# Layer 0, first convolution: two classes of row pairs interleaved in each frame, written in adjacent elements and read every second one

## The chip, the cores and the metric

The kernel runs as one program on one core of a Trainium2 chip. Its time is what the device takes for one execution, in microseconds (us). Five engines matter here: TensorE (PE in the profile; PEld is its weight load), VectorE (DVE), ScalarE (ACT), GpSimd (POOL) and SyncE (SP), which issues most DMA transfers. A difference of 0.2% of the time, about 10 us, can be told from no change.

## What is computed

A stack of four residual layers on `x`, shape (4, 16, 512, 512), float32. The change lies in layer 0, so only that layer is given in full:

```python
def _denoise_block(x, w1, b1, w2, b2, w3, b3, a, b, c):
    trip = _triplets(x)                      # frames t-1, t, t+1 (mirrored at the ends)
    B, T, C, H, W = trip.shape
    xf = trip.reshape(B * T, C, H, W)
    o = a * _conv_reflect(xf, w1, b1, 1, 2) + b * _conv_reflect(xf, w2, b2, 2, 4) \
      + c * _conv_reflect(xf, w3, b3, 4, 8)  # three 5x5 convolutions, dilation 1, 2, 4
    return jnp.tanh(o).reshape(B, T, H, W)
...
x = x + denoise_block_2(denoise_block_1(_gn(x)))   # layer 0
x = x + conv3x3(quantized(_gn(x)))                 # layer 1
x = x + box17x17(_gn(x))                           # layer 2
x = x + irfft2(complex_conv3x3(rfft2(_gn(x))))     # layer 3
```

`_gn` normalises groups of two of the sixteen frames (channels) over the whole image.

## The kernel before

Layer 0 is class `Layer0`. Its two convolutions (`conv` 0 and 1, blocks 1 and 2 of the reference) are worked as 32 groups: conv 0 for the four batches, four output frames at a time, then conv 1 in the same way. A group takes six slots, one for each of the six products over time: six combinations `v[q]` of the input frames are formed on VectorE (`early`, `late`; lines 487 to 551), each is convolved in space on TensorE (`products`, line 579), and the six results are combined into four output frames (`gather`, lines 626 to 647). The 96 slots of conv 0 come first, the 96 of conv 1 after them. `slot` writes the order by hand: TensorE's products of a slot, then on the other engines the results of the slot before, and the frames and combinations that the next group needs. Every engine works its list in that order.

**A frame** is a tile of 128 partitions by 2376 elements (line 87, ten of them, taken from a list of free ones). A patch of 2 rows by 16 columns stands in 32 partitions; the image's four quarters (128 rows each) stand in the four groups of 32 partitions. Along the free axis of a conv 0 frame there are 33 column blocks `k` of 72 elements. The 64 row pairs of a quarter are sorted by their number modulo 4 into four classes of 16, and each class has one more element at either end, the rim, which holds the row pair of the neighbouring quarter: 4 x 18 = 72.

**Making a conv 0 frame** is `x_frame`. For each half `h` of the frame's rows, ScalarE normalises the raw rows into `xp` (line 399) and mirrors 8 columns at each side (lines 400, 401); VectorE transposes blocks of 32 x 32 from `xp` into the frame (line 432, 1056 elements in each partition). In such a block a partition's number in its quarter is `2m + u`, with `m` from 0 to 15 and `u` 0 or 1, so one transpose delivers two classes, `u` = 0 and 1, of the half `h`. ScalarE then copies the rims from the transposed tile `ek`, 132 elements for each side (line 436). A group of conv 0 makes four frames, the first of a batch five: 64 frames in all, 128 transposes.

**The products** read the frames. One product takes a pair of displacements `d`, `d + 1` (in row pairs); for each column block its moving operand is two runs of 16 elements, one of the class that `d` leads to and one of the class of `d + 1`, for 16 column blocks: 16 x 2 x 16 = 512 columns. `source` gives the address. `PAIRS` lists five `d` whose two weight blocks lie side by side, so that one product fills 64 output columns (32*64 in the profile, "wide" below); `ALONE` lists the displacements that are worked 32 columns at a time (32*32, "narrow"), two of them beside each other. The four groups of partitions (`i`) and two halves of the columns (`j`) run as separate tiles of the array at once: eight wide instructions or sixteen narrow ones fill it. Each float32 product is two instructions in the profile. A slot thus has 160 wide and 128 narrow instructions, wide first in even slots and narrow first in odd ones, so that two slots together have 40 rounds of eight wide ones in a row.

Conv 1 has frames of another layout, loaded by DMA (`y_frame`); there the runs are 32 elements long.

Of the kernel before, what the change touches and what calls it, by code (L numbers as in the profile page):

```python
# [122 lines left out]
class Layer0:  # L123
# [299 lines left out]
    def x_frame(self, b, t, raws, ek, f):  # L423

        nc = self.nc
        fr = self.free.pop(0)
        v = fr.rearrange("p (k u c m) -> p k u c m", u=2, c=2, m=18)
        scale, bias, _ = self.gn[b]
        for h in range(2):
            raw = raws[h].rearrange("p (s w) -> p s w", s=2)  # L430
            xp = self.normalised(raw, scale[:, t : t + 1], bias[:, t : t + 1], f"{b}_{t}_{h}")
            nc.vector.transpose(v[:, :, :, h, 1:17].rearrange("p k u m -> p k m u"), xp)  # L432
        rim = ek.rearrange("p k (e f m) -> p k e f m", e=2, f=4)
        v = fr.rearrange("p (k q m) -> p k q m", q=4, m=18)
        for side in range(2):
            nc.scalar.copy(v[:, :, :, 17 * side], rim[:, :, side, f, :])
        return fr

    def y_frame(self, gr, i, t):
# [119 lines left out]
    def products(self, gr, p):  # L559
        nc, conv, q = self.nc, gr["conv"], ORDER[p]  # L560
        ps = self.psum.tile([P, 4, 512], F32, name=f"m{self.now}", tag="m")
        v = gr["v"][q]
        w = self.w[q]
        runs = [(e, pair) for e in range(2) for pair in PAIRS], [(e, two) for e in range(2) for two in ALONE]
        order = [(wide, *what) for wide in ((1, 0) if p % 2 == 0 else (0, 1)) for what in runs[1 - wide]]

        def source(i, d, k, j):
            if conv:
                a = [1188 * (c % 4 // 2) + 66 * (c % 2) + 1 + c // 4 for c in (d, d + 1)]
                first, step, nk, nm = 132 * k + 32 * j, 132, 8, 32  # L570
            else:
                a = [18 * (c % 4) + 1 + c // 4 for c in (d, d + 1)]
                first, step, nk, nm = 72 * (k + 16 * j), 72, 16, 16
            o = v[PX * i : PX * i + PX]
            return bass.AP(o.tensor, o.offset + first + a[0], [o.ap[0], [step, nk], [a[1] - a[0], 2], [1, nm]])

        def product(at, i, weights, d, e, j, n):
            nc_ = 8 if conv else 16
            return nc.tensor.matmul(  # L579
                ps[at, i, :].rearrange("p (k c m) -> p k c m", k=nc_, c=2),  # L580
                w[PX * i : PX * i + PX, weights],
                source(i, d, e, j),
                start=(n == 0),
                stop=(n == len(order) - 1),
                skip_group_check=True,
            )

        for n, (wide, e, what) in enumerate(order):
            base = len(DELTA) * PX * e
            for i in range(4):  # L590
                for j in range(2):
                    if wide:
                        d, o = what
                        at = base + PX * o
                        ins = product(slice(64 * j, 64 * j + 64), i, slice(at, at + 64), d, e, j, n)
                        continue
                    for u, (d, o) in enumerate(what):
                        at = base + PX * o
                        out = slice(64 * j + PX * u, 64 * j + PX * u + PX)
                        ins = product(out, i, slice(at, at + PX), d, e, j, n)  # L600
            self.marks.append(ins.ins)
        gr["m"][q] = ps
# [1187 lines left out]
```

## Time and profile before

| What | Value |
|---|---|
| time, median of 3 runs | 5083.87 us (5082.6 to 5091.45) |
| time of the profiled execution | 5071.62 us |
| its span on the core | 5069.8 us |
| ACT busy | 2564.1 us (51%) |
| products of layer 0 (L579), PE busy | 2610.4 us in 55296 instructions |
| combining frames (L487, 128x2376), DVE busy | 607.9 us in 232 instructions |
| transposes into the frames (L432), DVE busy | 261.6 us in 128 instructions |
| rim copies (L436), ACT busy | 43.5 us in 128 instructions |
| DMA: read, written | 497.51 MB, 340.03 MB |

The span covers the profiled execution from its first to its last instruction; the 1.8 us that the execution takes beyond it lie around the program. The profiled execution was 12.3 us faster than the median of the runs. Busy times of an engine are sums over the whole span; conv 0 of layer 0 takes roughly the first 28% of it, conv 1 the next 27%. In a line of instruction groups the shape is partitions x elements, `x128` the number of instructions, then the sum of their busy time in us, the mean of one in ns, and the idle time before them with what ended it.

### The profile page before, as it was taken

The page shows a single profiled execution, that of the slowest core. Times are in us where ns is not written, and L with a number is a line of the kernel's source. Part 1 is how long each engine was busy: PE and PEld are TensorE (multiplying, and loading weights), DVE is VectorE, ACT ScalarE, POOL GpSimd, SP SyncE. Part 2 cuts the span into 40 slices and gives each one's busy share as a digit, 9 for nine tenths or more (in the row PEclk, how much of TensorE's full clock was granted, in tenths as well). Part 3 has the DMA queues.
Part 4 walks back from the last instruction along what each step waited for, and adds up shares of the span by engine and source line. Part 5 has one row for each costly group of instructions (what it writes and reads, how often), then busy time and mean ns, then how long its engine had stood idle before and what let it go on. Part 6 is the DMA issues. An engine that isn't in the chain of part 4 may idle for free.

```text
span 5069.8 us, 209515 instructions
## 1 busy us (share of the span) xinstructions
PE 4765.5 (94%) x94320; PEld 2775.5 (55%) x94320; DVE 4070.7 (80%) x4639; ACT 2564.1 (51%) x4220; POOL 21.4 (0%) x90
## 2 busy tenths in 40 slices
PE   4899999999999989999999699989999989999999
PEld 1344444444554434444444456558888857777776
DVE  8988888979689999999998565555555588888887
ACT  3455656563224443534443555445444456666665
POOL 0000000000000000000000000000000000000000
PEclk9999999999999999999999899999999989999999
DMA  5655655564567776877774777776666655555553
GB/s 173 164 163 160 178 162 162 150 167 103 124 144 162 148 153 153 169 153 149 167 155 116 218 232 240 228 232 216 214 215 211 200 136 150 142 148 148 143 151 114
DMA packets 393857, 851.22 MB, mean 168 GB/s; under 512 B 70912, under 2 KB 86400, under 8 KB 384512
## 3 DMA queue, kind: packets, MB, share of 16 engines
q1 hardware_dynamic: 385456, 827.22, 61.0%
q8 instruction: 739, 12.11, 1.1%
q10 hardware_dynamic: 7504, 10.60, 0.8%
q14 instruction: 158, 1.29, 0.1%
HBM read 497.51 MB, written 340.03 MB: 165 GB/s over the span
## 4 chain that ended last, share of the span: by engine, by line
PE 78%; DVE 14%; issue 3%; DMA 2%; ACT 2%; SPq 1%; ACTq 0%; POOL 0%; DVEq 0%
PE m L579 39%; PE l1p L1044 11%; PE l2p L1151 8%; PE u L1619 5%; PE s L1560 5%; PE u L1560 4%; DVE frame L487 4%; PE u L1582 2%; PE pt L1594 2%; DVE frame L432 2%; DVE l2o L1191 2%; PE l2p L1202 1%; DVE st L1192 1%; DVE B L630 1%; DVE A L631 1%
## 5 line engine op out<-in xcount | busy, mean ns | idle before, releaser
L579 PE MATMUL m<-frame,l0w 32*64 32x512 f32 (+1 forms) x55296 | 2610.4, 610 | 174.8 <-DVE frame L527 63.4
L579 PEld LDWEIGHTS m<-frame,l0w 32*64 32x64 f32 (+1 forms) x55296 | 1193.9, 119 | 1590.4 <-issue 1361.8
L487 DVE SCALAR_TENSOR_TENSOR frame<-frame,frame 128x2376 f32<-128x2376 f32 x232 | 607.9, 2628 | 8.6
L1044 PE MATMUL l1p<-l1q,l_wt 32*32 32x512 f32 x12288 | 481.3, 601 | 64.6 <-DVE l1q L1034 40.4
L1044 PEld LDWEIGHTS l1p<-l1q,l_wt 32*32 32x32 f32 x12288 | 263.0, 103 | 229.2 <-issue 151.1
L1191 DVE TENSOR_TENSOR l2o<-l2x,l2p 128x512 f32<-128x512 f32 x256 | 172.7, 675 | 267.0 <-PE l2p L1151 267.0
L712 ACT ACTIVATE junk<-xb,neg 128x1024 f32<-128x1024 f32 x256 | 293.6, 1147 | 82.8 <-DVE top L691 36.5
L1151 PEld LDWEIGHTS l2p<-k_c_band,l2y 128*128 128x128 f32 x2048 | 256.8, 190 | 76.0 <-issue 55.2
L1180 ACT COPY l2y<-l2p 128x512 f32<-128x512 f32 x256 | 149.9, 586 | 284.2 <-PE l2p L1151 284.2
L1151 PE MATMUL l2p<-k_c_band,l2y 128*128 128x144 f32 (+1 forms) x2048 | 284.3, 292 | 6.1
L432 DVE STREAM_TRANSPOSE frame<-xp 128x1056 f32<-128x1056 f32 x128 | 261.6, 2128 | 31.1 <-ACT xp L401 31.1
L1151 PE MATMUL l2p<-k_c_band,l2n 128*128 128x144 f32 (+1 forms) x2048 | 269.7, 292 | 13.7 <-ACT l2n L1169 10.4
L1151 PEld LDWEIGHTS l2p<-k_c_band,l2n 128*128 128x128 f32 x2048 | 263.0, 197 | 14.7 <-ACT l2n L1169 10.9
L1061 DVE BATCH_NORM_STATS2 l1st<-l1o 128x6 f32<-128x512 f32 x256 | 158.2, 681 | 135.0 <-ACT l1o L1059 134.9
L1059 ACT ACTIVATE l1o<-l1p,k_l_bias,l_osc 128x1024 f32<-128x1024 f32 x128 | 147.2, 1200 | 233.6 <-PE l1p L1044 227.8
L1619 PE MATMUL u<-k_c_hil,zt 128*128 128x128 f32 x2048 | 255.9, 278 | 0.0
L1619 PEld LDWEIGHTS u<-k_c_hil,zt 128*128 128x128 f32 x2048 | 238.4, 192 | 2.1 <-issue 0.8
L1595 ACT COPY zt<-pt 128x512 f32<-128x512 f32 x256 | 131.4, 599 | 209.5 <-PE pt L1594 209.5
L1525 DVE TENSOR_TENSOR xc<-l3n,k_c_tab 128x2048 f32<-128x2048 f32 x64 | 146.7, 2293 | 106.6 <-ACT l3n L1509 106.6
L1638 DVE SCALAR_TENSOR_TENSOR l3o<-u,l3t 128x256 f32<-128x256 f32 x512 | 192.2, 426 | 22.2 <-ACT l3t L1630 19.5
L1044 PE MATMUL l1p<-l1x,l_wt 32*32 32x512 f32 x4088 | 194.6, 597 | 0.0
L1630 ACT ACTIVATE l3t<-u,rr 128x128 f32<-128x128 f32 x512 | 152.3, 362 | 70.3 <-DVE rr L1613 53.5
(314 smaller groups left out, 6351.3 us busy)
## 6 DMA issues: line engine op xcount, KB each, us to landing
y<-y SPq DMA_DIRECT2D x256, 264.0 KB
xb<-in_x SPq DMA_DIRECT2D x512, 128.0 KB
x<-l1o SPq DMA_DIRECT2D x256, 256.0 KB
l2x<-x SPq DMA_DIRECT2D x64, 1024.0 KB
x<-l2o SPq DMA_DIRECT2D x64, 1024.0 KB
l3x<-x SPq DMA_DIRECT2D x256, 256.0 KB
out<-l3o SPq DMA_DIRECT2D x256, 256.0 KB
l1x<-x SPq DMA_DIRECT2D x252, 256.0 KB
```

The costliest lines, as they stand in the source:

```text
L432: nc.vector.transpose(v[:, :, :, h, 1:17].rearrange("p k u m -> p k m u"), xp)
L487: self.nc.vector.scalar_tensor_tensor(o, x, f, y, ALU.mult, ALU.add)
L579: return nc.tensor.matmul(ps[at, i, :].rearrange("p (k c m) -> p k c m", k=nc_, c=2), w[PX * i : PX * i + PX, weights], source(i, d, e, j) ...
L712: nc.scalar.activation(junk, xs[h], f, bias=neg, accum_out=self.out_sums[b][n][:, 2 * t + h : 2 * t + h + 1])
L1044: ins = nc.tensor.matmul(ps[32 * j : 32 * j + 32, b, :], wt[rows, a, d], qs[v % 3][rows, k, d : d + W] if d < 3 else raws[v][rows, k], sta ...
L1061: nc.vector.bn_stats(st[b][:, u, :], o[:, b, :])
L1151: nc.tensor.matmul(ps[:, lo:hi], lhs[:, k, at : at + P], band[:, j : j + hi - lo], start=(k == 0), stop=(k == 3), skip_group_check=True,)
L1191: nc.vector.tensor_add(o[:, hb, :], xt[:, hb, :], ps)
L1560: nc.tensor.matmul(ps[b][32 * j : 32 * j + 32], f[rows, n, j, :], x[rows, j, :], start=(i == 0), stop=(i == 2 and tag == "s"), skip_group_ ...
L1619: nc.tensor.matmul(po[:, bass.ts(k, P)], zt[:, b, k ^ 1, :], hil[:, k, :], start=False, stop=(k == 3), skip_group_check=True,)
L1630: nc.scalar.activation(t[:, cols], po[:, cols], AF.Identity, bias=rr[:, b, odd : odd + 1], scale=0.5)
L1638: nc.vector.scalar_tensor_tensor(o[:, v].rearrange("p k u -> p u k"), po[:, HW:W].rearrange("p (u k) -> p u k", u=2), s, t.rearrange("p (u ...
```

## The change

Two classes that differ in `u` now alternate element by element: a column block of 72 elements is 2 (`c`, the half `h`) x 18 (`m`) x 2 (`u`), where it was 2 (`u`) x 2 (`c`) x 18 (`m`). A transpose therefore writes 32 adjacent elements for each column block, where it alternated between two places 36 elements apart. The rim copies write to the same two ends, in the new order. A conv 0 product reads each of its runs of 16 with a step of two elements (`sm`), from start addresses that follow the new layout. Conv 1 keeps its step of one. The sums on VectorE work on whole frames and are the same.

```diff
@@ x_frame
-        v = fr.rearrange("p (k u c m) -> p k u c m", u=2, c=2, m=18)
+        v = fr.rearrange("p (k c m u) -> p k c m u", c=2, m=18, u=2)
...
-            nc.vector.transpose(v[:, :, :, h, 1:17].rearrange("p k u m -> p k m u"), xp)
+            nc.vector.transpose(v[:, :, h, 1:17].rearrange("p k m u -> p k (m u)"), xp)
         rim = ek.rearrange("p k (e f m) -> p k e f m", e=2, f=4)
-        v = fr.rearrange("p (k q m) -> p k q m", q=4, m=18)
         for side in range(2):
-            nc.scalar.copy(v[:, :, :, 17 * side], rim[:, :, side, f, :])
+            to = v[:, :, :, 17 * side].rearrange("p k c u -> p k u c")
+            nc.scalar.copy(to, rim[:, :, side, f, :].rearrange("p k (u c) -> p k u c", u=2))
@@ products, source
             if conv:
                 a = [1188 * (c % 4 // 2) + 66 * (c % 2) + 1 + c // 4 for c in (d, d + 1)]
-                first, step, nk, nm = 132 * k + 32 * j, 132, 8, 32
+                first, step, nk, nm, sm = 132 * k + 32 * j, 132, 8, 32, 1
             else:
-                a = [18 * (c % 4) + 1 + c // 4 for c in (d, d + 1)]
-                first, step, nk, nm = 72 * (k + 16 * j), 72, 16, 16
+                a = [36 * (c % 2) + 2 + 2 * (c // 4) + c % 4 // 2 for c in (d, d + 1)]
+                first, step, nk, nm, sm = 72 * (k + 16 * j), 72, 16, 16, 2
             o = v[PX * i : PX * i + PX]
-            return bass.AP(o.tensor, o.offset + first + a[0], [o.ap[0], [step, nk], [a[1] - a[0], 2], [1, nm]])
+            return bass.AP(o.tensor, o.offset + first + a[0], [o.ap[0], [step, nk], [a[1] - a[0], 2], [sm, nm]])
```

The instructions of every engine, their number and their order are the same before and after; only addresses and steps differ.

## The prediction

> **What bounds the kernel now.** I read the page's first lines, then the stretches of conv 0, the waits of TensorE in it, the chain of waits, and last the weight loads in order of time, since a matmul's reading rate is what the change touches.
>
> ```profile
> span 5069.8 us, 209515 instructions
> PE 4765.5 (94%) x94320; PEld 2775.5 (55%) x94320; DVE 4070.7 (80%) x4639; ACT 2564.1 (51%) x4220; POOL 21.4 (0%) x90
> ...
> 423.30:756.20 332.90, 322.77 (x6920) 152.14 (x6919) 289.37 (x227) 195.85 (x333) 4.72 (x20) 0.98 0.59 164
> 756.20:1088.70 332.50, 320.82 (x6923) 144.87 (x6915) 289.15 (x227) 195.81 (x333) 4.74 (x20) 0.99 0.58 164
> ...
> PE m L579 <- DVE frame L527: 63.4, 1, 63.4
> PE m L579 <- DVE frame L487: 34.2, 11, 6.8
> ```
>
> The middle rows are two batches of conv 0, 24 slots each: PE busy 97% of them, DVE 87%. The waits (total, times, longest) say that PE starts at 63.4 us, after the first frames, and later stands still mostly for combinations of frames that VectorE brings late. So TensorE sets the pace, with VectorE close behind. How fast can TensorE go when nothing is late? The weight loads show it; each is issued as the round before it starts to stream, so from row to row is the time of one round of eight wide instructions:
>
> ```profile
> 1000.42 0.23 PEld L579 LDWEIGHTS m<-frame,l0w 32*64 32x64 f32 x16 [0.90 <-issue]
> ...
> 1003.05 0.18 PEld L579 LDWEIGHTS m<-frame,l0w 32*64 32x64 f32 x8 [0.25 <-issue]
> 1003.48 0.18 PEld L579 LDWEIGHTS m<-frame,l0w 32*64 32x64 f32 x8 [0.25 <-issue]
> 1003.91 0.18 PEld L579 LDWEIGHTS m<-frame,l0w 32*64 32x64 f32 x8 [0.25 <-issue]
> 1004.38 0.17 PEld L579 LDWEIGHTS m<-frame,l0w 32*64 32x64 f32 x8 [0.29 <-issue]
> 1004.84 0.17 PEld L579 LDWEIGHTS m<-frame,l0w 32*64 32x64 f32 x8 [0.29 <-issue]
> ...
> 1018.05 0.29 PEld L579 LDWEIGHTS m<-frame,l0w 32*32 32x32 f32 x32 [0.88 <-issue]
> ...
> 1026.91 0.23 PEld L579 LDWEIGHTS m<-frame,l0w 32*64 32x64 f32 x16 [0.89 <-issue]
> ```
>
> Two slots take 26.49 us (1000.42 to 1026.91): 40 wide rounds in 17.63, 16 narrow ones in 8.86. Hence 13.24 us a slot, 96 x 13.24 = 1271 us. Conv 0 really lasts from 63.4 to 1417.7 (its last matmul), 1354 us: 83 us are lost to late frames and the half clock after them.
>
> The rows show a second thing. Rounds take 0.43 us, but the two that start at 1003.91 and 1004.38 take 0.47 and 0.46: those of the pair `d` = 1. Over all slots, from the starts of the matmuls, I get 0.464 for `d` = 1 and 0.429 for the other four; in conv 1 it is 0.448 for `d` = 2, 0, 1 and 0.4285 for 4 and -2. Same columns, same weights' size: only addresses differ. Cut the frame's rows into blocks of four elements. Runs of `d` = 1 go from 19 to 34, then 37 to 52, next 91: at each step of `k` two blocks that give one element each follow one another. In conv 1 the slow three have the same once for each `k`. Where a block gives two elements between full ones (`d` = 4, -2) nothing is lost. So two lone elements cost 35 ns / 16 = 2.2 ns in conv 0, 20 / 8 = 2.5 in conv 1. An element takes 0.4285 / 512 = 0.837 ns; if a block needs a time T, then 2 x (T - 0.837) = 2.2 to 2.5 and T = 1.94 to 2.09 ns.
>
> **The change part by part.** *Reading.* No matmul of the trace takes two elements from each block throughout, which is what all conv 0 products will do. The nearest rows are ScalarE's, at about the same time an element (L1028: 1232 ns for 1024, 812 for 512, so 0.82):
>
> ```profile
> L360 ACT ACTIVATE xs<-xs,xshift 128x1024 f32<-128x1024 f32 x96 | 109.2, 1137 | 1.1
> L1509 ACT ACTIVATE l3n<-l3d,own_l 128x1024 f32<-128x1024 f32 x64 | 83.0, 1297 | 0.0
> L436 ACT COPY frame<-ek 128x132 f32<-128x132 f32 x128 | 43.5, 445 | 0.0
> ```
>
> L1509 reads every second element of the same 1024; it takes 160 ns more over 512 blocks, 0.31 for each: T = 1.67 + 0.31 = 1.98 ns. (Its fastest, 1182 ns, would give 1.76.) L436 writes one element to a block: against the copy of 16 elements at L400 (205 ns) it is (445 - 205) / 116 = 2.07 ns. Three different readers and writers agree on about 2 ns a block. I take 1.98, the row nearest in pattern; the bounds are 1.67 (two elements hide a block) and 2.09.
>
> The Trainium skill, page "Advanced Engine Details and Errata", section "SBUF Cachelines", states 16-byte lines and that two hits on a line absorb the access latency. L1509 here disagrees with it by those 160 ns; by the rule alone the sum would be rival B's.
>
> New starts follow from `a`: 36 (c % 2) + 2 + 2 (c // 4) + (c % 4) // 2. For `d` = 4 and -2 they are 0 or 1 modulo 4: eight blocks of two a run. For 2, 0 and 1 they are 2 or 3: nine blocks, with a lone element at both ends. An instruction has 32 runs: 256 x 1.98 = 507 ns (+80) or 288 x 1.98 = 570 (+143; for `d` = 1, which has lost 35 already, +108). Two instructions each, and two halves `e`: wide 4 x (2 x 80 + 2 x 143 + 108) = 2216 ns a slot. Narrow: the pair (-4, 6) has only full runs, +80; (-1, 3) one run of each kind, (80 + 143) / 2 - 16 lost already = +95; 4 x 175 = 700 ns. But 16 narrow rounds take 8.86 us where 16 x 0.4285 = 6.86 would do, so something else slows about half of them and can hide half of this: 350 to 700, I take 500. Together +2.7 us a slot, x 96 = +259 us.
>
> *Transposes.* 128 of them, now against the other transpose of 1056 elements with the same source pattern, which writes adjacent elements:
>
> ```profile
> L432 DVE STREAM_TRANSPOSE frame<-xp 128x1056 f32<-128x1056 f32 x128 | 261.6, 2128 | 31.1 <-ACT xp L401 31.1
> L420 DVE STREAM_TRANSPOSE ek<-xp_r 128x1056 f32<-128x1056 f32 x20 | 25.6, 1279 | 66.9 <-ACT xp_r L401 66.9
> ```
>
> 0.85 us each, 109 us of VectorE's time. What of it counts is bounded by the chain of waits: in the first 1420 us L432 is 6.5% of it, 92 us, so at most 92 x 0.4 = 37 us, and the half clock that goes with those waits. At the start eight transposes precede the first matmul; behind them ScalarE's L399 to L401 need 1.65 us a half, more than the new 1.28, so I count 4 us, not 7. In the slots the list of VectorE falls from 12.1 us (1164 us of conv 0 over 96) to 11.1 while PE's grows to 15.9: the 83 us of lateness go but for some 8 in the first, fullest slots: -75.
>
> *Rims.* 128 copies still send each element to a block of its own: 445 ns, no change, under ScalarE's idle half (ACT 195.85 of 332.90). Nothing else moves; no DMA, no queue, no wait is added. VectorE's work behind `m` (`gather`) starts later with the slots, and PE is its only waiter.
>
> Sum: +259 - 75 - 4 = +180 us on the span of 5069.8, which the execution exceeds by 1.8: 5252 us. The median of the runs lay 12.3 above that execution: about 5264.
>
> **The rivals.**
>
> *B, two elements hide a block* (not slower). For it: two-element blocks between full ones cost nothing in either convolution. Against it: they may live on slack from the full neighbours, and L1509 has no such neighbours. Then T = 1.67 and only lone ends cost: 288 x 1.67 = 480, +53. Wide 4 x (2 x 53 + 18) = 496, narrow 4 x 11 = 44: +0.54 us a slot, +52 us. Lateness falls from 83 to 25 (in a stall of 10 us some five transposes save 4, and eight slots longer by 0.54 another 4; the first ten slots keep 21). 52 - 58 - 4 = -10: 5074. It decides for T below about 1.69 (0.1 ns of T is some 50 us). If lone ends cost nothing either (*C*), the slots stay at 13.24, lateness falls to 44, and it is -43: 5041; `d` = 1 and conv 1 speak against it.
>
> *D, the streams share* (much slower). Narrow rounds read four streams from the same partitions. The densest now, (-1, 3), takes 0.917 us for two rounds: four streams of ten blocks a `k`, 40 in 28.6 ns, 1.4 a ns. If that is a ceiling, 64 to 72 blocks need 46 to 51 ns, 731 or 777 ns (68 in the mean) an instruction: 4 x (289 + 319) - 380 hidden = 2.1 us a slot instead of 0.5. With T = 1.98 it gives 5264 + 154 = 5418, with 2.09 in the wide rounds as well (+0.6 us a slot) 5476. For it: the spread of L1509, 1182 to 1449 ns. Against it: narrow rounds of plain runs of 512 in layer 3 (L1560) take 0.60 us, no less than these, so that reading need not be their limit.
>
> *E, the transposes don't gain.* L420 writes whole rows, these leave gaps of four elements. But at 15.9 us a slot VectorE at 12.1 is not late: no more than 10 us on the forecast. Cover for B, not for A.
>
> **How the numbers follow.** Forecast A (T 1.9 to 2.1, 5210 to 5345): 0.55. Between A and B (L1509's 1.76): 0.06. B 0.17, half of it above 5074. C 0.07. D 0.15. The time is A's, 5264. The range leaves out C, the lowest of B and the half of D above 5418: 5062 to 5420. Faster by over 0.2% (below 5074): C and half of B, 0.16; within 0.2%: 0.05; slower: 0.79. By 0.2%, some 10 us, this kernel's runs can be told apart.
>
> **What would show it.** L432 at about 1.28 us. Wide rounds of conv 0 in two kinds: 0.51 for `d` = 4 and -2, 0.57 for 2, 0 and 1; two slots in 31.9 us. PE nearly always busy, its waits for L487 in conv 0 a few us; conv 1's rounds unchanged. Rounds of 0.43 and 0.48 would be B; narrow rounds far over 0.6 would be D. I am wrong altogether if TensorE fetches far ahead and the rounds stay at 0.43.

## The result, and the profile after

| | before | after |
|---|---|---|
| median of the runs taken side by side | 5083.24 us (4 runs) | 5141.75 us (4 runs) |
| ratio, 95% interval | 1 | 1.0115 [1.0099, 1.0131] |
| span of the profiled execution | 5069.8 us | 5140.5 us |
| conv 0, first to last matmul of it | 63.4 to 1417.3 us | 59.9 to 1478.0 us |
| conv 1 | 1366.8 us | 1367.6 us |

The change makes the kernel slower by 58 us, where 180 were forecast. In the profiled executions conv 0's last matmul is 60.7 us later; conv 1 is the same, and the rest is 9 us longer. That rest is the same work in every kernel here; before's profiled execution has the shortest of the nine traces (2285 us, the others 2288 to 2303, after 2294) and lay 12 us under the median of its runs, so these 9 us are a spread between executions.

The page of after, its first lines and the chain that ended last (shares by engine), and one group:

```profile
span 5140.5 us, 209515 instructions
...
PE 4880.4 (95%) x94320; PEld 2838.6 (55%) x94320; DVE 3974.7 (77%) x4639; ACT 2562.8 (50%) x4220; POOL 21.5 (0%) x90
...
PE 87%; DVE 7%; DMA 2%; issue 2%; ACT 1%; SPq 0%; ACTq 0%; DVEq 0%
...
L579 PE MATMUL m<-frame,l0w 32*64 32x512 f32 (+1 forms) x55296 | 2723.0, 631 | 123.6 <-DVE frame L527 59.9
```

VectorE is busy 96 us less (4070.7 before), TensorE 115 us more. The same number of matmuls takes 2723 us instead of 2610. The saving and the cost have both come; the saving was on an engine that sets the pace only where a frame is late. The stretches of the second and third batch (length; busy time of PE, PEld, DVE, ACT, POOL with instructions; granted clock, DMA share, GB/s) and the waits of TensorE in conv 0 (total, times, longest) show it:

```profile
425.60:776.40 350.80, 350.80 (x6920) 163.71 (x6912) 265.34 (x227) 195.40 (x334) 4.75 (x20) 1.00 0.56 155
776.40:1127.40 351.00, 351.00 (x6927) 161.94 (x6919) 265.28 (x227) 195.47 (x334) 4.75 (x20) 1.00 0.57 155
```

```profile
PE m L579 <- DVE frame L527: 59.9, 1, 59.9
PE m L579 <- issue: 5.0, 1, 5.0
PE m L579 <- DVE frame L487: 3.5, 1, 3.5
```

A batch takes 351 us instead of 333, TensorE is busy in all of it at full clock, and VectorE falls from 87% of the stretch to 76%. The waits for L487, 34.2 us before, are down to one of 3.5. So all of these batches is now time of TensorE's rounds: 24 slots of 13.25 us would have been 318 us before, of 14.61 us they are 351, and the 15 us a batch of late frames are gone. The weight loads in order of time, from row to row one round of eight wide instructions (the first row of a run of wide rounds, nine later ones, and the start of the narrow ones and of the next pair of slots):

```profile
1058.90 0.23 PEld L579 LDWEIGHTS m<-frame,l0w 32*64 32x64 f32 x16 [0.97 <-issue]
1059.42 0.17 PEld L579 LDWEIGHTS m<-frame,l0w 32*64 32x64 f32 x8 [0.29 <-issue]
1059.88 0.17 PEld L579 LDWEIGHTS m<-frame,l0w 32*64 32x64 f32 x8 [0.29 <-issue]
1060.38 0.18 PEld L579 LDWEIGHTS m<-frame,l0w 32*64 32x64 f32 x8 [0.33 <-issue]
1060.89 0.18 PEld L579 LDWEIGHTS m<-frame,l0w 32*64 32x64 f32 x8 [0.33 <-issue]
1061.40 0.18 PEld L579 LDWEIGHTS m<-frame,l0w 32*64 32x64 f32 x8 [0.33 <-issue]
1061.91 0.18 PEld L579 LDWEIGHTS m<-frame,l0w 32*64 32x64 f32 x8 [0.33 <-issue]
1062.38 0.17 PEld L579 LDWEIGHTS m<-frame,l0w 32*64 32x64 f32 x8 [0.29 <-issue]
1062.84 0.17 PEld L579 LDWEIGHTS m<-frame,l0w 32*64 32x64 f32 x8 [0.29 <-issue]
1063.34 0.17 PEld L579 LDWEIGHTS m<-frame,l0w 32*64 32x64 f32 x8 [0.33 <-issue]
...
1078.73 0.33 PEld L579 LDWEIGHTS m<-frame,l0w 32*32 32x32 f32 x32 [1.00 <-issue]
...
1088.17 0.23 PEld L579 LDWEIGHTS m<-frame,l0w 32*64 32x64 f32 x16 [0.97 <-issue]
```

There are two kinds of rounds, as forecast, but at 0.46 and 0.51 us, not 0.51 and 0.57. Two slots take 29.27 us (1058.90 to 1088.17; 26.49 before, 31.9 forecast): 19.83 for the 40 wide rounds (17.63), 9.44 for the narrow ones (8.86). Medians over all slots, from the starts of the matmuls: 0.465 for `d` = 4 and -2, 0.508 for 2 and 0, 0.498 for 1. The rounds of conv 1 stay at 0.4285 and 0.4485.

In the groups (busy time in us and mean in ns, then the idle time before them) the transposes are where they were forecast, and the rim copies are 11 ns longer (445 before); the row of L1509 is the group from which the price of a block was taken:

```profile
L432 DVE STREAM_TRANSPOSE frame<-xp 128x1056 f32<-128x1056 f32 x128 | 161.7, 1272 | 88.9 <-ACT xp L401 88.9
...
L1509 ACT ACTIVATE l3n<-l3d,own_l 128x1024 f32<-128x1024 f32 x64 | 83.6, 1306 | 0.0
...
L436 ACT COPY frame<-ek 128x132 f32<-128x132 f32 x128 | 44.5, 456 | 0.0
```

### The profile page after: what moved, and what is told of

The parts are those of the page before. It is cut to its first block, busy times and chain, and to the rows that moved or that the text cites. A ratio compares the mean times of both kernels' runs of the same rounds, so it can differ in the third digit from the quotient of the medians.

```text
span 5140.5 us, 209515 instructions
## 1 busy us (share of the span) xinstructions
PE 4880.4 (95%) x94320; PEld 2838.6 (55%) x94320; DVE 3974.7 (77%) x4639; ACT 2562.8 (50%) x4220; POOL 21.5 (0%) x90
## 4 chain that ended last, share of the span: by engine, by line
PE 87%; DVE 7%; DMA 2%; issue 2%; ACT 1%; SPq 0%; ACTq 0%; DVEq 0%
PE m L579 49%; PE l1p L1044 11%; PE l2p L1151 8%; PE u L1619 5%; PE s L1560 5%; PE u L1560 4%; PE u L1582 2%; PE pt L1594 2%; DVE l2o L1191 2%; PE l2p L1202 1%; DVE st L1192 1%; DVE frame L487 1%; DMA frame<-y 1%; DVE zr L686 0%; PE pr L1604 0%
## 5 line engine op out<-in xcount | busy, mean ns | idle before, releaser
L579 PE MATMUL m<-frame,l0w 32*64 32x512 f32 (+1 forms) x55296 | 2723.0, 631 | 123.6 <-DVE frame L527 59.9
L579 PEld LDWEIGHTS m<-frame,l0w 32*64 32x64 f32 (+1 forms) x55296 | 1250.7, 119 | 1594.9 <-issue 1372.1
L487 DVE SCALAR_TENSOR_TENSOR frame<-frame,frame 128x2376 f32<-128x2376 f32 x232 | 607.7, 2628 | 8.6
L432 DVE STREAM_TRANSPOSE frame<-xp 128x1056 f32<-128x1056 f32 x128 | 161.7, 1272 | 88.9 <-ACT xp L401 88.9
```

The costliest lines, as they stand in the source:

```text
L432: nc.vector.transpose(v[:, :, h, 1:17].rearrange("p k m u -> p k (m u)"), xp)
L487: self.nc.vector.scalar_tensor_tensor(o, x, f, y, ALU.mult, ALU.add)
L579: return nc.tensor.matmul(ps[at, i, :].rearrange("p (k c m) -> p k c m", k=nc_, c=2), w[PX * i : PX * i + PX, weights], source(i, d, e, j) ...
```

## The experiments

All are edits of one of the two kernels. "Lateness" is the time from conv 0's first matmul to conv 1's first, less 48 times the time of two slots in which nothing is late.

### The reads alone

The frames, and the transposes that write them, as before; only `source` is that of the change, so TensorE multiplies elements that stand for other rows.

```diff
 # before, source
-                a = [18 * (c % 4) + 1 + c // 4 for c in (d, d + 1)]
-                first, step, nk, nm = 72 * (k + 16 * j), 72, 16, 16
+                a = [36 * (c % 2) + 2 + 2 * (c // 4) + c % 4 // 2 for c in (d, d + 1)]
+                first, step, nk, nm, sm = 72 * (k + 16 * j), 72, 16, 16, 2
```

> Before with the address pattern of the changed kernel in the products of conv 0 alone: the frames keep their old layout, so the products of conv 0 read the wrong elements, as many and in the same time pattern as the changed kernel. Theory R: rounds as in the changed kernel (0.464 for d = 4 and -2, 0.51 for 2 and 0, 0.50 for 1), two slots 29.2 us, +130 us of streaming, lateness from 83 to 30 to 40 because TensorE is slower: 5083 + 130 - 48 = 5165 (5150 to 5180), so the transposes give the changed kernel some 20 us. Rival W (the changed kernel's slower rounds come from the new frames' writes, not from the reads): rounds of 0.43, time 5083.

Measured: 5159.07 us, ratio 1.0130 [1.0108, 1.0152]. The rounds are the ones of after to the nanosecond (0.465, 0.507, 0.509, 0.498), two slots 29.2 us. One batch of it, and the waits:

```profile
425.60:776.40 350.80, 350.24 (x6907) 159.85 (x6907) 290.65 (x227) 195.76 (x331) 4.73 (x20) 1.00 0.55 155
```

```profile
PE m L579 <- DVE frame L527: 64.1, 1, 64.1
PE m L579 <- issue: 12.2, 2, 9.0
PE m L579 <- DVE frame L487: 8.3, 5, 5.5
```

So the cost is the reading, and nothing else of the change. The stretch shows more: VectorE is as busy as before (290.65 us; 289.37), its transposes are as slow, and yet TensorE hardly waits. The longer slots alone let VectorE keep up but for the first ten slots, where 26 of the 30 us of lateness are.

### The transposes alone, rows out of order

Here a transpose writes two runs of 16 adjacent elements, one for each class, with loads and reads as before. The row pairs of a quarter then stand in another order than the products assume: what is computed differs, the work is the same.

```diff
 # before, x_frame
-            nc.vector.transpose(v[:, :, :, h, 1:17].rearrange("p k u m -> p k m u"), xp)
+            nc.vector.transpose(v[:, :, :, h, 1:17], xp)
```

> The kernel before, with the transposes of conv 0 writing two runs of 16 adjacent elements into the frames; loads and TensorE's reads stay as before (one transfer of 32 partitions, step one). The rows of each quarter lie in another order in the frame than the products assume, so the output isn't the reference's; the amount of work is the same. Theory (transposes' gain alone, reads cost nothing when unchanged): a transpose 1.28 us instead of 2.13, wide rounds .429 as before, PE's waits on the frames down from 83 us of lateness to 35-50, time 5036-5055 (-30 to -50). With the run of the reads alone (+66 to +76) this would leave the change at +20 to +45, or lower if the cover of longer rounds makes the lateness vanish for reads alone too. Rival V (the frames are late for something other than the transposes): no change, 5075-5095.

Measured: 5050.55 us, ratio 0.9931 [0.9916, 0.9945], -35 us. The group of the transposes, one batch, the waits:

```profile
L432 DVE STREAM_TRANSPOSE frame<-xp 128x1056 f32<-128x1056 f32 x128 | 161.3, 1272 | 60.6 <-ACT xp L401 60.6
```

```profile
406.70:732.00 325.30, 320.79 (x6920) 152.46 (x6912) 264.69 (x227) 195.01 (x334) 4.73 (x20) 0.99 0.60 167
```

```profile
PE m L579 <- DVE frame L527: 60.7, 1, 60.7
PE m L579 <- DVE frame L487: 21.8, 5, 4.6
PE m L579 <- issue: 10.8, 2, 9.4
```

With the rounds at 0.429 the batch takes 325.3 us instead of 332.9, and the lateness is 48 us instead of 83. This is the gain that the change aimed at; it exists. Together with the runs of after and of the reads alone it gives all four corners:

| | ratio to before | lateness of conv 0 | 48 times two slots |
|---|---|---|---|
| before | 1 | 82.6 us | 1271.7 us |
| transposes alone | 0.9931 [0.9916, 0.9945] | 48.3 | 1271.6 |
| reads alone | 1.0130 [1.0108, 1.0152] | 30.1 | 1402.5 |
| both (after) | 1.0115 [1.0099, 1.0131] | 16.2 | 1402.2 |

Quicker transposes take 34 us of lateness away while the rounds are quick, and 14 when they are slow (by the ratios, whose intervals overlap, the latter can't be told from nothing). The parts don't add up: 1.0130 x 0.9931 = 1.006 would be +31 us, inside the +20 to +45 expected of that sum; measured are +58. What the slower rounds cost (131 us), they partly cover themselves (52 us of lateness), and with it most of what the transposes had to give. Each lateness is that of one traced execution.

### Five ways of reading

In after's kernel each of the five `d` of the wide products of conv 0 gets a pattern of its own, all from aligned starts and with 512 elements; the results are no convolution.

```diff
 # after, source, conv 0
+                ap = {
+                    4: [[72, 16], [36, 2], [1, 16]],   # adjacent, 128 blocks
+                    2: [[72, 16], [4, 16], [1, 2]],    # two adjacent of four, 256 blocks
+                    0: [[72, 16], [36, 2], [2, 16]],   # step two, 256 blocks
+                    -2: [[72, 16], [24, 2], [3, 16]],  # step three, 384 blocks
+                    1: [[72, 16], [4, 2], [4, 16]],    # step four, 512 blocks
...
```

> The changed kernel, but every wide product of conv 0 reads 512 elements in a pattern of its own, all starting on a block of four: d = 4 step one; d = 2 two adjacent elements of every block; d = 0 step two; d = -2 step three (384 blocks); d = 1 step four (512 blocks); narrow ones step two. The products of conv 0 are therefore of wrong elements. Theory T (a block costs the reader about 1.81 ns whatever is taken from it, hidden only behind more than two elements): rounds of 0.43, 0.464, 0.464, 0.695 and 0.927 us. Rival P (the price is the step, not the block): d = 2 at 0.43. Rival M (a further block costs 1.35 ns, as the lone ends in the changed kernel: 44 ns for 32 of them): 0.464 + 128 x 1.35 = 0.637 for step three, 0.464 + 256 x 1.35 = 0.81 for step four.

Measured in one execution: 5298.66 us. The weight loads of this kernel, in order of time; the patterns come in the order of the list, two rounds each:

```profile
905.46 0.23 PEld L586 LDWEIGHTS m<-frame,l0w 32*64 32x64 f32 x16 [0.90 <-issue]
905.94 0.18 PEld L586 LDWEIGHTS m<-frame,l0w 32*64 32x64 f32 x8 [0.25 <-issue]
906.37 0.18 PEld L586 LDWEIGHTS m<-frame,l0w 32*64 32x64 f32 x8 [0.25 <-issue]
906.82 0.17 PEld L586 LDWEIGHTS m<-frame,l0w 32*64 32x64 f32 x8 [0.27 <-issue]
907.26 0.17 PEld L586 LDWEIGHTS m<-frame,l0w 32*64 32x64 f32 x8 [0.27 <-issue]
907.72 0.17 PEld L586 LDWEIGHTS m<-frame,l0w 32*64 32x64 f32 x8 [0.29 <-issue]
908.18 0.17 PEld L586 LDWEIGHTS m<-frame,l0w 32*64 32x64 f32 x8 [0.29 <-issue]
908.85 0.19 PEld L586 LDWEIGHTS m<-frame,l0w 32*64 32x64 f32 x8 [0.49 <-issue]
909.53 0.19 PEld L586 LDWEIGHTS m<-frame,l0w 32*64 32x64 f32 x8 [0.49 <-issue]
910.43 0.20 PEld L586 LDWEIGHTS m<-frame,l0w 32*64 32x64 f32 x8 [0.72 <-issue]
911.35 0.20 PEld L586 LDWEIGHTS m<-frame,l0w 32*64 32x64 f32 x8 [0.72 <-issue]
```

The first row loads for two rounds, so the first pattern shows one distance. The distances are 0.43, 0.45 and 0.44, twice 0.46, 0.67 and 0.68, 0.90 and 0.92. From the starts of the matmuls:

| pattern | blocks | round, us | ns a block |
|---|---|---|---|
| adjacent | 128 | 0.4285 | 3.35 (four elements of 0.837) |
| two adjacent of four | 256 | 0.4445 | 1.74 |
| step two | 256 | 0.462 | 1.80 |
| step three | 384 | 0.674 | 1.76 |
| step four | 512 | 0.908 | 1.77 |

From 256 blocks on the time goes with the number of 16-byte blocks, at 1.74 to 1.80 ns each. So the mechanism of the forecast holds, a price per block that shows once an instruction takes less than 1.8 ns worth of elements from it; the price was set at 1.98. The expected 0.464, 0.695 and 0.927 of theory T are met within 5%, where M's 0.637 and 0.81 are missed. One point stays between the theories: two adjacent elements take 0.4445, midway between P's 0.43 and T's 0.464. They are 18 ns quicker than two with a gap, so at two elements to a block the gap makes about half of the 34 ns that step two costs; why is open.

The same rows speak against rival B. The Trainium skill, page "Advanced Engine Details and Errata", section "SBUF Cachelines", says that at least two hits on a 16-byte line are needed to absorb the access latency. Here two are not enough: two elements of 0.837 ns fall just short of the block's time, 0.462 us against 0.4285, 8% more.

### One stream instead of two

In after's kernel the second half of the columns (`j` = 1) is left out for `e` = 1, so that each group of partitions sends one stream, not two, through the array. A part of the output isn't computed.

```diff
 # after, products
-                for j in range(2):
+                for j in range(2 if conv or e == 0 or n == len(order) - 1 else 1):
```

> The changed kernel without the products of the second half of the columns (j = 1) in the second half of each slot's list (e = 1), apart from the last product: there only one stream reads a group of partitions in wide rounds, and two in narrow ones, instead of two and four. That work is left out. Theory T (each stream pays for its own blocks): wide rounds of e = 1 as those of e = 0, 0.464 and 0.50 to 0.51. Rival S (streams share the partition's reads): wide rounds of e = 1 at 0.43, or markedly nearer to it, narrow ones of e = 1 likewise.

Measured in one execution: 5121.15 us. The weight loads of wide rounds with one stream (four instructions a round):

```profile
1058.76 0.17 PEld L579 LDWEIGHTS m<-frame,l0w 32*64 32x64 f32 x4 [0.33 <-issue]
1059.23 0.17 PEld L579 LDWEIGHTS m<-frame,l0w 32*64 32x64 f32 x4 [0.30 <-issue]
1059.69 0.17 PEld L579 LDWEIGHTS m<-frame,l0w 32*64 32x64 f32 x4 [0.30 <-issue]
1060.20 0.17 PEld L579 LDWEIGHTS m<-frame,l0w 32*64 32x64 f32 x4 [0.34 <-issue]
1060.70 0.17 PEld L579 LDWEIGHTS m<-frame,l0w 32*64 32x64 f32 x4 [0.34 <-issue]
```

0.47, 0.46, 0.51, 0.50: the same with half the streams. In wide rounds the price is one of each stream by itself, not of streams that share the memory. Rival D was about the narrow rounds, four streams to a group of partitions: in after they grew by 0.29 us a slot where D needed 2.1. By the starts of the matmuls, where wide rounds come first in the slot, the pair (-4, 6) takes 0.4745 us in the first half of the list in after (0.4415 before) where D needed 0.731. The same pair in the second half of the list takes 0.54 before and 0.56 after, but 0.47 here with two streams. So something does slow half of the narrow rounds in both kernels, and goes with half the work left out; whether it is the streams or the number of instructions stays open.

### Rows put in order by the load, three ways

If the raw rows came into the partitions sorted by `u`, the transposes could write adjacent elements and TensorE read adjacent ones. The first try reorders within each transfer:

```diff
 # before, load_half; the transposes as in the run with rows out of order
-        n = PX if self.marks else P
+        n = PX
...
-            self.move(xt[r : r + n], src[r : r + n])
+            self.move(xt[r : r + n], src[r : r + n].rearrange("(m u) w -> u m w", u=2))
```

> The layout of before (each class in 16 adjacent elements, TensorE reads with a step of one), but the raw rows of conv 0 are loaded so that partition 16u + m of a quarter holds what 2m + u held; so a transpose writes two runs of 16 adjacent elements. Nothing is left out. Theory R (all of the loss is TensorE's reading, and VectorE's gain is worth what lateness it takes away): L432 at 1.28 us, rounds as before (0.429, and 0.464 for d = 1), two slots 26.5 us, lateness of conv 0 from 83 us to about 44, so -43 us: 5041 (5020 to 5060). Rival V (VectorE's time is not worth anything, lateness has another cause): 5083 +- 5, lateness still about 80 us. The loads of the first frames are four transfers each instead of one; if the start is late for it, the first matmul comes after 63 us and that is seen there.

Measured: 6576.21 us, ratio 1.2916 [1.2890, 1.2942]. A miss, but not of the transposes (1278 ns) nor of the rounds (0.429). The first matmul starts at 161.5 us instead of 63.4. One stretch of its conv 0, and the wait of ScalarE for raw rows in the first 3000 us:

```profile
400.00:2900.00 2500.00, 1296.06 (x25727) 544.46 (x25743) 980.69 (x828) 673.41 (x1123) 17.17 (x74) 0.74 0.25 78
```

```profile
ACT xp L399 <- DMA xr<-in_x: 658.7, 76, 48.7
```

The DMA engines move 78 GB/s at a mean share of 0.25, where before it was 153 at 0.57 in conv 0; ScalarE waits 659 us for rows. The transfers have become slow though few engines' time is used. The Trainium skill, page "DMA: Bandwidth & Descriptors", section "Rules for kernel authors", says that an outermost dimension smaller than 16 confines a transfer to so many of the engines, and here it is `u`, 2. The share and the rate agree with that; the profile shows only the mean over the engines, not which of them worked. The second try, whose loads have 16 rows outermost, moves 165 GB/s again (400 to 1000 us, mean share 0.64), which fits.

The second try keeps plain transfers, two of 16 partitions for each one of 32 (five frames that wait in the pool from the start of the kernel keep the old way):

```diff
 # before, load_half
+            for u in range(2) if apart else ():
+                at = r + 16 * u
+                self.move(xt[at : at + 16], src[r + u : r + n : 2])
```

> As e1, but each permuted load of 32 partitions is two transfers of 16 rows (the rows with u = 0, then those with u = 1), instead of one whose outermost dimension is u; and the five frames that are loaded before anything else keep their old loads and old transposes (10 of 128). The products read with a step of one, as before. Nothing is left out. Theory R: 118 transposes at 1.28 us, 10 at 2.13; rounds as before (0.429; 0.464 for d = 1), two slots 26.5 us; lateness of conv 0 from 83 us to about 44 to 50, start unchanged: 5083 - 36 = 5047 (5035 to 5062), below both kernels. Rival V (lateness does not come from the transposes' time): 5083 +- 8. Rival Q (472 more transfers in SyncE's queue make loads late): waits of ScalarE for xr grow as in e1, time above 5083. With e2 (reads alone, +76 us against before) and the changed kernel (both, +58) this makes the third corner: if the parts did not touch each other, it would be 58 - 76 = -18.

Measured: 5124.16 us, ratio 1.0058 [1.0044, 1.0071], slower than before, as rival Q had it. Waits in conv 0 (line numbers four or five higher):

```profile
ACT xp L403 <- DMA xr<-in_x: 55.7, 21, 9.8
```

```profile
PE m L584 <- DVE frame L492: 46.7, 12, 9.2
```

Before, ScalarE waited 3.1 us for these rows, TensorE 34.2 for L487. With rows that late the quicker transposes (168.3 us in all instead of 261.6) bring nothing, and the lateness is 108 us.

The third try brings the number of transfers back to that of before: both halves of an image share a tile, and 8 transfers of 16 partitions bring 8 KB in one piece to each; three such pairs take the place of six halves.

```diff
 # before; load_x for the rows of conv 0 becomes
+            src = self.a["x"][b, t].rearrange("(J m u q) w -> J u m (q w)", J=4, m=16, u=2)
+            for n in range(8):
+                to = both[16 * n : 16 * n + 16].rearrange("p T w -> p (T w)")
+                self.move(to, src[n // 2, n % 2])
```

> The same adjacent writes with the rows in the right order: two halves of an image share a pair of 8 KB tiles and are loaded in 8 transfers of 16 partitions with 8 KB in one piece each, so that the transposes write adjacent runs and TensorE reads step one. Computes the reference. Theory: transposes 1.28 us, wide rounds .429, 5045-5055 (-30 to -40) if transfers are as punctual as before. Rival (larger buffers given back later and 16-partition transfers make loads late): waits on the loads over 40 us and 5083 or more.

Measured: 5085.91 us, ratio 0.9998 [0.9984, 1.0012]: no change, though neither expectation is met as put. Waits in conv 0 and one batch (lines nine or ten higher):

```profile
ACT xp L408 <- DMA xs<-in_x: 32.0, 6, 15.1
...
ACT xp L408 <- DMA xr<-in_x: 3.6, 1, 3.6
```

```profile
437.70:766.10 328.40, 321.90 (x6920) 151.65 (x6912) 264.49 (x227) 195.25 (x334) 4.73 (x20) 0.99 0.74 166
```

The rows are now in time in the steady batches: 328, 330 and 326 us instead of 333, 332.5 and 329. But the first batch takes 374 instead of 360, with ScalarE standing still for 27 of these 36 us before it normalises rows, and that gives it back. The DMA engines' share is 0.74 for 166 GB/s, where before it was 0.59 for 164. Why 16-partition pieces take more of it, and whether a fourth pair of tiles would mend the first batch, was not tried. So no version here beats the kernel before with the right rows; the 35 us of the run with rows out of order show what such a version could gain.

## Why the prediction was right in direction and wrong in size

| Step | forecast | measured |
|---|---|---|
| wide round, `d` = 4, -2 | 0.507 us | 0.465 |
| wide round, `d` = 2, 0 (and 1) | 0.570 | 0.508 (0.498) |
| wide rounds, more a slot | 2.22 us | 1.10 |
| narrow rounds, more a slot | 0.5 us | 0.29 |
| 96 slots | +259 us | +130.5 (1402.2 - 1271.7) |
| lateness | -75 us | -66.4 (82.6 to 16.2) |
| start | -4 us | -3.5 |
| last matmul of conv 0 | +180 us | +60.7 |

*The price of a block* is the step that failed: "I take 1.98, the row nearest in pattern". It is a term of the right kind and the wrong size. The wide rounds with two elements to a block give 464.5 / 256 = 1.81 ns, and the five patterns 1.74 to 1.80. With 1.81 for every block the forecast's own formula makes 4 x (2 x 35 + 2 x 93 + 58) = 1256 ns of the wide rounds of a slot instead of 2216: 92 us less of the 128 that were too many. The number came from another engine, and that engine's time depends on more than the pattern. L1509 has two groups in the trace of before, with the same reads; the first takes one operand more (min, median and max in ns):

```profile
L1509 ACT ACTIVATE l3n<-l3d,l3twice,own_l x64: 1321/1387/1497, 4074.3 to 5026.4; 128x1024 f32<-128x1024 f32 x64
L1509 ACT ACTIVATE l3n<-l3d,own_l x64: 1182/1286/1449, 4075.5 to 5027.7; 128x1024 f32<-128x1024 f32 x64
```

The groups lie some 100 ns apart and each spreads by more than that, while the whole price was read from 160 ns against L360, an instruction with other operands. And of the two other rows that "agree on about 2 ns", one was a writer, the other a difference of lone elements. The fastest of the second group, named in the prediction and given 0.06, makes 1.76, inside what the patterns measured; the fastest of the first makes 2.03 by the same sum. So that 1.76 lies so near is luck as far as these runs show. With it the forecast would have been 4 x (2 x 22 + 2 x 78 + 43) = 972 ns a slot, 93 us, and with at most 21 of the narrow rounds and its -75 and -4 a sum of +14 to +35 us, too low in turn.

*Lone ends.* A run of nine blocks was to cost nine times the price. It takes 0.508 us: 43 ns for 32 more blocks, 1.35 ns each. For the three pairs with such runs that is 4 x 39 = 156 ns a slot less than with 1.81, 15 us. Before, two lone elements in a row cost 2.2 ns more than two of a stream; the cost of a block's edge is not one number, and what sets it stays open.

*Narrow rounds.* +0.29 instead of 0.5 us a slot, 20 us: this fits the price again, by which the formula for them shrinks from 700 to 330 ns, of which half to all was to count. The three differences, 92, 15 and 20, make up the 128. (In the forecast's formula 507 and 570 lie 78 and 142 above 428.5, not 80 and 143; that is 3 us of the 259.)

*Transposes and lateness.* 1.27 us each, as taken from L420. VectorE's time for them fell by 100 us (261.6 to 161.7), not 109, which was no term of the sum. The lateness fell by 66, not 75, and nearly all of the 16 us left are in the first ten slots, where 8 were expected. The reason given, that longer slots and quicker transposes together make it go, fits the four corners: the longer slots alone take 52 us of it, the quicker transposes alone 34, both 66. How much of the 66 is due to which can't be said, since the shares depend on which comes first.

*The rivals.* B (two elements hide a block) and C fall by the rounds of after and by the five patterns. D falls by the narrow rounds of after, 0.29 us a slot more instead of 2.1. E, that the transposes gain nothing, falls by their 1272 ns in after; the run with rows out of order shows they gain 35 us where there is something to gain. The time came out between A and B, a case that got 0.06. That was far too little while the price stood on one group of another engine whose own spread reached that far.

## What to carry to other kernels

Before a layout is turned for the writer's sake, look at what its readers pay: here a write that 128 instructions do was made 0.85 us cheaper, and 27648 matmuls of the engine that sets the pace, which read what it writes, came in rounds some 6 to 19% longer. Where the price of an access is taken from another engine's instruction, neither its mean nor its fastest is safe (here 1.98 or 1.76 by one group, 2.03 by the fastest of its twin): such a row gives a range, and one kernel with the pattern on the engine in question, as the five ways of reading, gives the price. Two gains against the same lateness don't add up: here what was late was cured by anything that gave it time, even by the slowdown itself.

## What the runs showed of the hardware

- In the wide rounds TensorE's reading of its moving operand (the matrix that streams through the array) took 1.74 to 1.80 ns for each 16-byte block from 256 blocks on: a round of 512 float32 columns takes 0.4285 us with adjacent elements, 0.462 at step two, 0.674 at step three and 0.908 at step four. At step two, runs that start 2 or 3 elements into a block take 0.508 instead of 0.465 us in after. One or two streams at once made no difference.
- Two adjacent elements of each block are read in 0.4445 us, two with a gap in 0.462, in the same number of blocks.
- VectorE's transpose of 128 x 1056 float32 took 1272 ns in the mean when it writes adjacent runs, of 32 or of 16 elements, and 2128 when it alternates between places 36 elements apart.
- The same rows loaded with an outermost dimension of 2 made the DMA engines move 78 GB/s instead of 153 in conv 0.
